# Gate and up projections from the third inner tile on by seven half-depth products instead of eight

## The chip, the cores and the metric

The kernel runs on one core of a Trainium2 chip. Times are device microseconds of one execution; the number that counts is the median of several executions. A profile of one further execution shows where its time went: TensorE (PE, and PEld for its weight loads), VectorE (DVE), ScalarE (ACT), GpSimd (POOL) and SyncE (SP, which only issues DMAs).

## What is computed

One transformer layer on 8 sequences of 128 tokens, width 512, all in float32:

```python
x = x + xattn(layernorm(x), ctx, ctx, mask, Wq, Wk, Wv, Wo)   # 32 heads, 8 kv heads of 128
x = x + ffn(layernorm(x), w1, w2, w3)

def ffn(x, w1, w2, w3):                     # w1, w2: [1376, 512], w3: [512, 1376]
    dq1, dq2, dq3 = (nf4_quant_dequant(w) for w in (w1, w2, w3))
    gate = einsum('bsd,hd->bsh', x, dq1)
    up = einsum('bsd,hd->bsh', x, dq2)
    return einsum('bsh,dh->bsd', silu(gate) * up, dq3)
```

`nf4_quant_dequant` scales each block of 64 weights by its largest absolute value, rounds to the nearest of 16 code values (15 bounds between them) and scales back. This quantizing is part of what the kernel computes.

## The kernel before

**Precision.** A float32 matrix product is made of three matmuls: each operand is split into a rounded high part (a cast on ACT, line 155) and a rest (a subtraction on DVE or POOL, line 156), and `product` (line 165) issues high x low, high x high and low x high for each 128-deep slice (line 172). A product over 512 input channels of a 128 x 512 result is thus 4 x 3 = 12 matmuls.

**The stages on PE.** First key and value projections and the first query projections (to about 118 us). Then 64 attention steps (line 762), a step being one sequence and one kv head with its four query heads. In each step PE does, in this order, a query product `pq` for a later unit, the output product `po` of three steps ago (line 700), the transposes of two steps ago (`turn`, line 696), the values of the step before (line 686) and this step's scores (line 675). From about 600 us on gate and up: for each of 11 tiles of the inner width (the last one padded) and each of 2 halves of the tokens, a product for gate and one for up (`gate_up`, line 730), then SiLU on ACT and a product on DVE (lines 751, 752) into `hT`. From 724 us on the down projection (line 872): for sequences 0 to 5 the inner tiles 0 to 7 first (`most`, 12 steps of 12 matmuls), then tiles 8 to 10 of these, then sequences 6 and 7. Its stationary operand `hs` is made from `hT` by `split_h` (line 841).

**The quantizing stream** runs beside all this. It is a Python generator (`quantize`, line 376) that issues the work of 17 units in order: 11 units of 128 x 1024 weights of w1 and w2 (`Up`), 5 such and one of 96 x 512 of w3 (`Down`). In a unit, each of the 15 bounds is a compare on ACT (line 196) and a sum on DVE into two PSUM banks (line 202); then a scaling on DVE. The next unit's weights are loaded by DMA some compares before the end (line 393) and normalized on POOL (line 206). `pump(n)` issues so many steps of the stream as its argument says, a step being 128 x 1024 wide; the calls stand by hand in the program (lines 645, 781, 799, 862, 886). What each engine then does, it does in the order in which the program issued it.

A finished `Up` unit leaves four 128 x 128 weight tiles in two stores: each splits 512 columns (ACT cast, POOL subtraction) and writes high and low part to DRAM (`store`, line 286). A finished `Down` unit leaves one or two w3 tiles that stay in SBUF (line 242). Such leftovers wait in a list and are issued one at a time by `store()` (line 411), once in each attention step, before its first `pump`. The gate/up tiles come back by DMAs from POOL's queue (`load_w12`, line 725) into six buffers that they share with the query weights and with `hs`.

**The order within an attention step** on ACT: two copies `rs_q` for the rope of the query product (lines 463, 464), the store's cast, the compares of `pump(1.5)`, the cast of the transposed values `aT`, tanh and exp of the scores (681, 682), the compares of `pump(1.65)`, the cast of a query or output weight tile. On DVE: the rope's product `rc_q` (465), sums of the first pump, `acc` (705), the rest of `aT`, reciprocal and scaling of the values (693, 694), sums of the second pump. On POOL: `rs_q`'s product (466), the store's subtraction, the mask product (684), the rope's sum (467), the subtraction of the weight tile.

**PSUM** has eight banks of 512 columns: two for the stream's sums, two (tag q) in turn for query products and transposes, two for the values, one for the scores, one for the output product.

Of the kernel before, what the change touches and what calls it, by code (L numbers as in the profile page):

```python
# [31 lines left out]
NG = 44  # L32

# [29 lines left out]
def block_kernel(ctx: ExitStack, tc: tile.TileContext, x, ctxt, mask, wq, wk, wv, wo, w1, w2, w3, w12t, w3_t,  # L63
# [6 lines left out]
    ps = ctx.enter_context(tc.tile_pool(name="ps", bufs=2, space=bass.MemoryType.PSUM))  # L70
    tp = ctx.enter_context(tc.tile_pool(name="tp", bufs=2))
    nf = ctx.enter_context(tc.tile_pool(name="nf", bufs=2))
# [7 lines left out]
    w12t_d = dram.tile([NHT, 2, P, 2, KT, P], F32, name="w12t_d")  # L80
# [31 lines left out]
    def rsqrt_apart(v, y, n, name):  # L112

        p = ps.tile([P, 1024], F32, tag="c", name=f"rp_{name}", bufs=1)
# [50 lines left out]
    def product(out, pairs, start=True, stop=True, high=False):  # L165


        n = len(pairs)
        for i, ((ah, al), (bh, bl)) in enumerate(pairs):
            three = [(ah, bh), (al, bh), (ah, bl)] if high else [(ah, bl), (ah, bh), (al, bh)]  # L170
            for j, (a, b) in enumerate(three):
                E.matmul(out, a, b, start=start and i + j == 0, stop=stop and i == n - 1 and j == 2)  # L172
# [11 lines left out]
    class Unit:  # L184
# [6 lines left out]
        def bound(self, i):  # L191
# [4 lines left out]
            S.activation(m, self.w, AF.Relu, bias=bias[:self.p, i:i + 1], scale=BIG if up else -BIG)  # L196
            step = float(NF4[i + 1] - NF4[i])
            if i == NEG[-1]:
                self.c = ps.tile([P, 1024], F32, tag="c", name=f"nc_{self.name}", bufs=1)[:self.p, :self.n]
# [48 lines left out]
    class Up(Unit):  # L248
# [30 lines left out]
        def finish(self):  # L279
            V.tensor_tensor(self.w, self.c, self.s, ALU.mult)  # L280
            for j, part in self.parts(self.w):
                for i in range(self.r // P):
                    fresh.append(lambda tag, h=self.start // P + i, j=j, src=part[:, :, i * P:(i + 1) * P]:
                                 self.store(h, j, src))

# [81 lines left out]
    ups = [Up((j,), h * P, 2 * P) for h in range(0, NHT - 1, 2) for j in range(2)] + [Up((0, 1), (NHT - 1) * P, P)]  # L367
# [8 lines left out]
    def quantize():  # L376
        invert = None
        for i, u in enumerate(units):
            for k, b in enumerate(NEG[::-1] + POS):
                u.bound(b)  # L380
# [9 lines left out]
                if k == 2:  # L390
                    u.begin()
                if i + 1 < len(units):
                    if k == (6 if isinstance(units[i + 1], Down) else 10):
# [23 lines left out]
    def end_store():  # L417
        if stored:
            stored.pop()()

# [6 lines left out]
    with ExitStack() as c1:  # L427
# [56 lines left out]
        with ExitStack() as c3:  # L484
# [61 lines left out]
            def masks():  # L546
# [5 lines left out]
                some = tp.tile([P, T], F32, tag="t_some", name="some", bufs=1)  # L552
# [6 lines left out]
                def count():  # L559
                    pa = bank("s", "pa")  # L560
# [162 lines left out]
        w12, hT, ups = {}, {}, []  # L723

        def load_w12(h):
            w12[h] = [wp.tile([P, 2, KT, P], F32R, tag="wq", name=f"w12_{h}_{j}", bufs=6) for j in range(2)]
            for j in range(2):
                nc.gpsimd.dma_start(w12[h][j], w12t_d[h, j])

        def gate_up(half, h, pool=None, between=None):  # L730
            t = xT2[half]
            pg, pu = bank("q", f"pg_{half}_{h}"), bank(("pv", "wo")[len(ups) % 2], f"pu_{half}_{h}")
            ups.append(h)

            def one(w, p):
                product(p, [((w[:, 0, k], w[:, 1, k]), (t[:, 0, k], t[:, 1, k])) for k in range(KT)])

            one(w12[h][0], pg)
            if between:
                between()  # L740
            one(w12[h][1], pu)
            if h % 4 == 0:
# [3 lines left out]
                else:  # L746
                    hT[half, h // 4] = pool.tile(shape, F32, tag="hT", name=name, bufs=4)

            def later():
                sg = tp.tile([P, 512], F32, tag="t1", name=f"sg_{half}_{h}")  # L750
                S.activation(sg, pg, AF.Silu)
                V.tensor_tensor(hT[half, h // 4][:, h % 4], sg, pu, ALU.mult)
# [9 lines left out]
        for i in range(N):  # L762
# [36 lines left out]
            pump(1.65 if 2 < i < 58 else 2 if i == 58 else 1 if i < 2 else 0)  # L799
# [7 lines left out]
            if i >= 61:  # L807
                load_w12(i - 61)
# [16 lines left out]
        evac = gate_up(0, 0, between=lambda: project(N - 1))  # L825
        ln.sums(7)
        turned((4, 5), ("s", "wo"))
        ln.finish()
        xn.update({k: ln.rows(k, "t2") for k in (6, 7)})
        evac()  # L830
# [100 lines left out]
```

## Time and profile before

| | |
|---|---|
| median of 3 executions | 789.2 us (789.14 to 790.14) |
| the profiled execution's own time | 790.0 us |
| its span, first to last instruction | 788.2 us |
| granted TensorE clock, mean | 0.998 |
| PE busy, share of the span | 778.0 us, 99% |
| DVE, ACT, POOL busy | 627.9 (80%), 586.4 (74%), 466.4 us (59%) |
| gate/up stage, third product to last | 614.9 to 723.6 us |
| down projection | 723.6 to 785.0 us |

The page gives busy time, number of instructions and, for groups of like instructions, total, mean length and the idle time before them with what ended it. Lengths of matmuls overlap in it, so the pace of PE is read from the starts of its weight loads. An engine runs its instructions in order; an instruction that waits holds up all behind it on its engine.

### The profile page before, as it was taken

The numbers are of one execution on the slowest core, as the hardware profiler recorded it, in microseconds if no ns is written. First come the engines' busy times: TensorE is split into PE (matmuls) and PEld (weight loads), VectorE is DVE, ScalarE is ACT, GpSimd is POOL, SyncE is SP. The second block draws the span as 40 slices with busy tenths as digits, with TensorE's granted clock in tenths as the row PEclk, the third lists the DMA queues.
The fourth block names the chain that finished last, engine by engine and source line by source line (L and its number), as shares of the span: only waits on it lengthen the run. The fifth ranks groups of instructions, "written<-read, shape, count | busy, mean of one in ns | idle before, by whom it ended". The sixth has DMA issues, their size and how long they took to land. (4 is left out here: it accounts for less than half of the span.)

```text
span 788.2 us, 11198 instructions
## 1 busy us (share of the span) xinstructions
PE 778.0 (99%) x3737; PEld 627.3 (80%) x3737; DVE 627.9 (80%) x840; ACT 586.4 (74%) x821; POOL 466.4 (59%) x411
## 2 busy tenths in 40 slices
PE   8999998999999999999999999999999999999998
PEld 6788886778777878778787877888778888888877
DVE  5767777888888887888888878879878688888981
ACT  7358667989796978879797979898732678778840
POOL 3568544688787878777797877878652223232100
PEclk9999999999999999999999999999999999999999
DMA  7966735355437344526337432414133235652011
GB/s 228 300 195 195 214 105 154 108 143 176 89 121 206 135 107 121 174 55 218 103 100 203 131 94 94 125 65 134 43 119 107 57 108 157 186 162 53 5 54 54
DMA packets 73329, 102.44 MB, mean 130 GB/s; under 512 B 7832, under 2 KB 42840, under 8 KB 73272
## 3 DMA queue, kind: packets, MB, share of 16 engines
q1 hardware_dynamic: 70104, 90.19, 38.2%
q0 software_dynamic: 3168, 11.54, 4.7%
q8 instruction: 30, 0.49, 0.3%
q14 instruction: 27, 0.22, 0.1%
HBM read 79.32 MB, written 22.38 MB: 129 GB/s over the span
## 5 line engine op out<-in xcount | busy, mean ns | idle before, releaser
L202 DVE SCALAR_TENSOR_TENSOR nc_w<-nm_w,nc_w 128x1024 f32<-128x1024 bf16 (+1 forms) x238 | 284.6, 1196 | 60.2 <-ACT nm_w L196 49.8
L196 ACT ACTIVATE nm_w<-w_w,bias 128x1024 bf16<-128x1024 f32 (+1 forms) x255 | 276.2, 1115 | 14.9 <-DVE nc_w L202 7.9
L172 PE MATMUL pq<-xT,wq 128*128 128x512 f32 x768 | 209.3, 422 | 0.0
L172 PE MATMUL po<-wo,aT 128*128 128x512 f32 x768 | 190.1, 396 | 0.0
L172 PEld LDWEIGHTS pq<-xT,wq 128*128 128x128 f32 x768 | 143.9, 188 | 55.9 <-issue 24.4
L172 PEld LDWEIGHTS po<-wo,aT 128*128 128x128 f32 x768 | 143.8, 189 | 34.5 <-issue 2.9
L684 POOL TENSOR_TENSOR th<-th,mt 128x512 f32<-128x512 f32 x64 | 83.8, 1310 | 87.9 <-ACT th L682 80.0
L466 POOL TENSOR_TENSOR rs_q<-rs_q,sgnq 128x512 f32<-128x512 f32 x64 | 82.9, 1295 | 14.7 <-ACT rs_q L464 14.7
L681 ACT ACTIVATE th<-pl 128x512 f32<-128x512 f32 x64 | 38.3, 598 | 53.5 <-PE pl L678 51.3
L467 POOL TENSOR_TENSOR qr<-rc_q,rs_q 128x512 f32<-128x512 f32 x56 | 72.5, 1295 | 0.0
L691 PE MATMUL pv<-vt,th 128*128 128x129 f32 x512 | 67.9, 276 | 0.1
L678 PE MATMUL pl<-qr,krt 128*128 128x512 f32 x128 | 66.4, 601 | 0.0
L172 PE MATMUL pg<-xT,w 128*128 128x512 f32 x264 | 63.7, 390 | 0.0
L172 PE MATMUL pu<-xT,w 128*128 128x512 f32 x264 | 63.5, 389 | 0.0
L691 PEld LDWEIGHTS pv<-vt,th 128*128 128x128 f32 x512 | 62.2, 192 | 0.7 <-POOL th L684 0.7
L172 PE MATMUL pd<-w3t,hs 128*128 128x512 f32 (+3 forms) x297 | 60.8, 366 | 0.4 <-POOL w3t L156 0.4
L172 PEld LDWEIGHTS pd<-w3t,hs 128*128 128x128 f32 (+1 forms) x297 | 51.3, 189 | 9.9 <-POOL w3t L156 0.8
L206 POOL TENSOR_TENSOR w_w<-w_w,s_w 128x1024 f32<-128x1024 f32 (+1 forms) x17 | 39.6, 2329 | 33.0 <-DMA s_w<-scale_d 31.6
L172 PEld LDWEIGHTS pu<-xT,w 128*128 128x128 f32 x264 | 49.6, 188 | 10.3
L172 PEld LDWEIGHTS pg<-xT,w 128*128 128x128 f32 x264 | 49.3, 188 | 10.1
L156 POOL TENSOR_TENSOR w3t<-w_w,w3t 128x512 fp32r<-128x512 f32 (+1 forms) x11 | 17.2, 1564 | 65.7 <-ACT w3t L155 65.7
L155 ACT CAST aT<-pt_a 128x512 fp32r<-128x512 f32 x64 | 36.6, 571 | 24.9 <-PE pt_a L162 24.9
(119 smaller groups left out, 1103.7 us busy)
## 6 DMA issues: line engine op xcount, KB each, us to landing
w12t_d<-dqt SPq DMA_DIRECT2D x22, 512.0 KB
w<-w12t_d POOLq DMA_DIRECT2D x22, 512.0 KB, 4.6
s_w<-scale_d SPq DMA_DIRECT2D x40, 256.0 KB
raw_wq<-in_L_xattn_Wq SPq DMA_DIRECT2D x32, 256.0 KB
raw_wo<-in_L_xattn_Wo SPq DMA_DIRECT2D x32, 256.0 KB
s_w<-scale_d SPq DMA_DIRECT2D x86, 64.0 KB
ws<-in_L_ffn_w SPq DMA_DIRECT2D x20, 256.0 KB
w_w<-in_w12t SPq DMA_DIRECT2D x10, 512.0 KB
```

What stands on the lines that cost most here:

```text
L155: S.copy(hi, src)
L156: engine.tensor_tensor(lo, src, hi, ALU.subtract)
L172: E.matmul(out, a, b, start=start and i + j == 0, stop=stop and i == n - 1 and j == 2)
L196: S.activation(m, self.w, AF.Relu, bias=bias[:self.p, i:i + 1], scale=BIG if up else -BIG)
L202: V.scalar_tensor_tensor(self.c, m, step, self.c, ALU.min, ALU.subtract if i == POS[0] else ALU.add)
L206: Q.tensor_tensor(self.w, self.w, self.s, ALU.mult)
L466: Q.tensor_tensor(s, s, every(sgn), ALU.mult)
L467: return lambda: (engine or Q).tensor_tensor(dst, c, s, ALU.add)
L678: E.matmul(pl, krt[kv, u % 2][:, bb * T:(bb + 1) * T], qr[u][:, bb].rearrange("p g t -> p (g t)"), start=True, stop=True)
L681: S.activation(th, pl, AF.Tanh, scale=ATTN_MULT / CAP)
L684: Q.tensor_tensor(em[i], em[i], mt.unsqueeze(1).to_broadcast([P, G, T]), ALU.mult)
L691: E.matmul(pv[:, g, :HD + 1], em[i][:, g], vt[kv][:, b], start=True, stop=True)
```

## The change

For tiles 2 to 10 of the inner width (`H0 = 2`), gate and up of both token halves are taken as one product of 2 x 2 blocks: rows are gate and up (w1 and w2), the inner dimension is cut into two halves of 256 input channels, columns are the two token halves. Instead of eight block products it makes seven (the scheme of Strassen in the form with few sums): P1 = A11 B11, P2 = A12 B21, P3 = S4 B22, P4 = A22 T4, P5 = S1 T1, P6 = S2 T2, P7 = S3 T3, where A are blocks of the weights, S sums of them, B blocks of the normalized tokens and T sums of them. Each block product has 2 x 3 = 6 matmuls. Tiles 0 and 1 stay as they were.

- **Weights.** The stream's `Up` units are recut: two for tiles 0 and 1 as before, then one unit for each tile with w1 and w2 together. After scaling, such a unit makes S1 to S4 with four DVE sums of 128 x 256 and leaves four stores, two of them with sums in front. A store writes one or two blocks. An attention step may issue a second store, ahead of its second pump, which is 1.7 instead of 1.65.
- **Tokens.** T1 to T4 are made and split once, on DVE, POOL and ACT, ahead of and beside the first products of the stage.
- **Results.** PSUM is laid out anew when the gate/up stage begins: two banks x, two v, one y, one z. Products add onto banks that ACT has filled by copies, so that most sums are made in PSUM; ACT makes four copies and two SiLUs a tile, DVE two sums and a product, POOL a product.
- **Loads.** Weight blocks are loaded one at a time by DMAs from SP's queue as buffers come free.
- **Stream.** In `Down` units three of the 15 compares go to POOL. Loads and second scale loads of a unit are issued at other compares. Each block product has `pump(0.74)`, and there are new pumps of 1.5 and 2.2 at the start of the stage.
- **Down.** `split_h` subtracts on POOL instead of DVE; the order of `most` is all sequences for tiles 0 to 3, then all for 4 to 7, and two of its steps come ahead of the last two block products.

The diff's core:

```diff
+H0 = 2
+PAIRS = [("A11", "S1"), ("S2", "A12"), ("S3",), ("A22", "S4")]
...
-        def bound(self, i):
+        def bound(self, i, engine=S):
...
+            if engine is S:
+                S.activation(m, self.w, AF.Relu, bias=bias[:self.p, i:i + 1], scale=BIG if up else -BIG)
+            else:
+                Q.tensor_single_scalar(m, self.w, float(BOUNDS[i]), op=ALU.is_gt if up else ALU.is_le)
...
             V.tensor_tensor(self.w, self.c, self.s, ALU.mult)
+            if len(self.js) == 2:
+                self.combine()
+                return
...
+        def combine(self):
+            a11, a12, a21, a22 = (self.w[:, i * 256:(i + 1) * 256] for i in range(4))
+            s1 = self.s[:, :256]
+            def first(tag):
+                V.tensor_tensor(s1, a21, a22, ALU.add)
+                self.store_blocks(s1, "S1")
+            def third(tag):
+                V.tensor_tensor(a21, a11, a21, ALU.subtract)
+                V.tensor_tensor(a11, a22, a21, ALU.subtract)
+                V.tensor_tensor(a12, a12, a11, ALU.subtract)
+                self.store_blocks(self.w[:, :512], "S2", "S4")
+            fresh.extend([first, lambda tag: self.store_blocks(self.w[:, :512], "A11", "A12"), third,
+                          lambda tag: self.store_blocks(self.w[:, 512:], "S3", "A22")])
+        def store_blocks(self, src, *names):
+            n = len(names)
+            t = nf.tile([P, 2, 2, 2 * P], F32R, tag="nf_t", name=f"dqs_{self.name}_{names[0]}")
+            split(t[:, :n, 0], t[:, :n, 1], src.rearrange("p (i n) -> p i n", i=n), Q)
+            for i, name in enumerate(names):
+                c, at = PLACE[name]
+                nc.sync.dma_start(w12s_d[self.start // P - H0, c][:, at].rearrange("p i k c -> p i (k c)"),
+                                  t[:, i].bitcast(F32))
...
-    ups = [Up((j,), h * P, 2 * P) for h in range(0, NHT - 1, 2) for j in range(2)] + [Up((0, 1), (NHT - 1) * P, P)]
+    ups = [Up((j,), 0, H0 * P) for j in range(2)] + [Up((0, 1), h * P, P) for h in range(H0, NHT)]
...
-                u.bound(b)
+                u.bound(b, Q if isinstance(u, Down) and k % 5 == 2 else S)
...
-                if k == 2:
+                if k == (2 if isinstance(u, Down) else 8):
                     u.begin()
                 if i + 1 < len(units):
-                    if k == (6 if isinstance(units[i + 1], Down) else 10):
+                    if k == (6 if isinstance(units[i + 1], Down) else 11):
                         units[i + 1].load()
...
-            pump(1.65 if 2 < i < 58 else 2 if i == 58 else 1 if i < 2 else 0)
+            if i > 3 and len(to_store) > 1:
+                store()
+            pump(1.7 if 2 < i < 58 else 2 if i == 58 else 1 if i < 2 else 0)
...
-        split(t[:, 0, :n], t[:, 1, :n], hT[b // 4, i][:, :, b % 4 * T:b % 4 * T + T], V)
+        split(t[:, 0, :n], t[:, 1, :n], hT[b // 4, i][:, :, b % 4 * T:b % 4 * T + T], Q)
...
+    Q.tensor_tensor(w11, plain(B11[0]), plain(B11[1]), ALU.add)
+    Q.tensor_tensor(t4, plain(B21[0]), plain(B21[1]), ALU.add)
+    V.tensor_tensor(t1, plain(b12[0]), w11, ALU.subtract)
+    V.tensor_tensor(t1, t1, plain(b12[1]), ALU.add)
+    V.tensor_tensor(t2, plain(B22[0]), t1, ALU.subtract)
+    V.tensor_tensor(t2, t2, plain(B22[1]), ALU.add)
+    def split_t123():
+        split(T1[0], T1[1], t1, Q)
+        V.tensor_tensor(w11, t2, w11, ALU.subtract)
+        split(T2[0], T2[1], t2, V)
+        Q.tensor_tensor(t4, t4, t2, ALU.subtract)
+        for k in range(2):
+            split(T3[0][k], T3[1][k], w11[:, k], Q)
+    def split_t4():
+        split(T4[0], T4[1], t4, Q)
...
+        def P1(self):
+            block(self.h, "A11", "B11", self.x)
+            def later():
+                S.copy(y, self.x)
+        def P5(self):
+            block(self.h, "S1", "T1", self.v)
+        def P6(self):
+            block(self.h, "S2", "T2", self.x, False)
+            return lambda: S.copy(self.h0, self.x)
+        def P2(self):
+            block(self.h, "A12", "B21", y, False)
+            def later():
+                self.sg = self.silu(y, "0")
+        def P7(self):
+            block(self.h, "S3", "T3", self.x, False)
+            def later():
+                S.copy(z, self.x)
+                S.copy(self.h1, self.x)
+                V.tensor_tensor(self.h1, self.h1, self.v, ALU.add)
+                V.tensor_tensor(self.v, self.v, self.h0, ALU.add)
+        def P4(self):
+            block(self.h, "A22", "T4", z, False)
+            return lambda: V.tensor_tensor(self.h0, self.sg, z, ALU.mult)
+        def P3(self):
+            block(self.h, "S4", "B22", self.v, False)
+            def later():
+                sg = self.silu(self.v, "1")
+                Q.tensor_tensor(self.h1, sg, self.h1, ALU.mult)
...
+    slots = [(H0, "P1"), (0, "both"), (1, "both"), (H0, "P2"), (H0, "P6"), (H0, "P5"), (H0, "P7")]
+    for h in range(H0, NHT):
+        slots += [(h + 1, "P1"), (h + 1, "P5"), (h, "P4"), (h + 1, "P6"), (h, "P3"), (h + 1, "P2"), (h + 1, "P7")]
+    slots = [k for k in slots if k[0] < NHT]
+    slots[-2:-2] = [(NHT, "down")]
...
+    most = [(b, i) for i in range(2) for b in range(6)]
+    down = most + [(b, 2) for b in range(6)] + [(b, i) for b in range(6, B) for i in range(3)]
...
+        store()
+        pump({"both": 2.2, "down": 3}.get(what, 0.74))
+        for _ in range(frees.get((h, what), 0)):
+            if chunks:
+                load_chunk()
+            elif to_split:
+                split_h(*to_split.pop(0))
```

## The prediction

> **What bounds the kernel now.** I read the page first: engine shares and the costliest groups.
>
> ```profile
> PE 778.0 (99%) x3737; PEld 627.3 (80%) x3737; DVE 627.9 (80%) x840; ACT 586.4 (74%) x821; POOL 466.4 (59%) x411
> L172 PE MATMUL pg<-xT,w 128*128 128x512 f32 x264 | 63.7, 390 | 0.0
> L172 PE MATMUL pu<-xT,w 128*128 128x512 f32 x264 | 63.5, 389 | 0.0
> ```
>
> PE is full, so matmuls taken away count in full where nothing else sets the end. The mean of 389 ns is a pipelined length. The timeline of the gate/up stage gives the true pace:
>
> ```profile
> 647.43 2.68 PEld L172 LDWEIGHTS pg<-xT,w 128*128 128x128 f32 x12
> 650.15 2.68 PEld L172 LDWEIGHTS pu<-xT,w 128*128 128x128 f32 x12
> 652.87 2.68 PEld L172 LDWEIGHTS pg<-xT,w 128*128 128x128 f32 x12
> ```
>
> Twelve matmuls start every 2.72 us: 0.2267 us each. Next, the chain of work that ended last:
>
> ```profile
> 747.48 9.23 issue
> 756.71 1.60 POOLq L927
> 758.35 26.69 PE pd L172 x147
> ```
>
> At 758.35 PE resumes because GpSimd has just split the last w3 tile. So the quantizing stream (ScalarE compares, VectorE sums, GpSimd splits) ends level with PE, and a faster PE meets it. Last, busy times by stretch (columns: PE, PE loads, DVE, ACT, POOL) and one attention step from the timeline:
>
> ```profile
> 160.00:560.00 400.00, 400.00 (x1983) 320.39 (x1982) 335.68 (x437) 339.66 (x480) 315.61 (x258) 1.00 0.43 127
> 408.75 0.63 ACT L682 ACTIVATE th<-th 128x512 f32<-128x512 f32 x1
> 409.29 2.17 ACT L196 ACTIVATE nm_w<-w_w,bias 128x1024 bf16<-128x1024 f32 x2
> 409.46 1.31 POOL L684 TENSOR_TENSOR th<-th,mt 128x512 f32<-128x512 f32 x1 [0.49 <-ACT th L682]
> 409.79 0.69 DVE L694 TENSOR_TENSOR ad<-pv,rs 128x512 f32<-128x512 f32 x1
> 410.72 1.30 POOL L467 TENSOR_TENSOR qr<-rc_q,rs_q 128x512 f32<-128x512 f32 x1
> 412.60 0.58 ACT L464 COPY rs_q<-pq 64x512 f32<-64x512 f32 x1
> 413.26 0.69 DVE L465 TENSOR_TENSOR rc_q<-pq,cosq 128x512 f32<-128x512 f32 x1 [0.24 <-ACT rs_q L464]
> 415.19 0.19 PEld L172 LDWEIGHTS pq<-xT,wq 128*128 128x128 f32 x1 [0.24 <-issue]
> ```
>
> A step lasts 7.68 us (exp at 401.09 and 408.75). ACT idles 60 us over the 52 steps of the stretch, 1.16 each. But its order is fixed: the next q product (415.19) needs the bank that rc_q leaves at 413.95, and rc_q follows ACT's copies. By this timeline ACT may be late by 1.24 us; over the other steps the distance from rc_q's end to the next q product is 1.2 to 2.4, mean 1.8.
>
> **The change, part by part.**
>
> Matmuls. A tile of the inner width took 4 products of 12 (two token halves, gate and up) = 48; now 7 blocks of 6 = 42. Nine tiles (2 to 10): 54 x 0.2267 = 12.24 us less PE work, if nothing waits.
>
> The end. PE begins the stage's third product at 614.88 in both. Then: 63 blocks x 1.36 = 85.7, two gate-and-up pairs of the old kind 10.9, twelve down steps x 2.72 = 32.6, the first two w3 tiles of the next step 1.36: PE wants the last w3 tile at 745.4. The stream has 11 x 16 + 5 x 16 + 8 + 15 = 279 units. Counting the pump calls, 259 are issued when the slots end (716.9 with two down steps in them); 20 remain, 12 of full size and 8 of the half-size last unit. VectorE needs 12 x 1.235 (full sums, back to back in the timeline) + 15 x 0.745 + 0.68 (the 96x512 ones) = 26.7 us. It can start at about 719.2, after the last SiLU (0.6), one hs cast (0.6) and one compare (1.14) on ACT: 745.9. Then the cast (1.1) and GpSimd's split (1.6) of the last w3 tile: 748.7. PE waits 3.3 us there, and the 147 matmuls behind are the same. Gain: 758.35 - 748.7 = 9.65 us instead of 12.24.
>
> What that end needs is freed elsewhere: hs subtractions go from DVE (24 x 0.69) to GpSimd, 18 compares from ACT (15 x 1.14 + 3 x 0.72 = 19.3 us) to GpSimd, which was busy 30.5 of 109 us in this stage. The trace has no one-source compare on GpSimd: per 1024 columns the memset takes 0.97 and the two-source product 2.40; I take 1.7, 18 x 1.7 = 31 us, hidden in its idle time.
> [...]
>
> Copies and sums in the gate/up stage, per tile: ACT four copies (4 x 0.58) more than its two SiLUs, DVE three sums instead of two (+0.69), GpSimd one product (1.3). With 5.2 units pumped per 9.52 us, ACT is busy some 8.4, DVE 8.4. Every copy has two blocks (2.72 us) before PE needs it; ACT reaches the copy for z about 1.6 late after two compares, so it fits narrowly. Bound: 0 to 10 us, of which the first 3.3 only replace the wait at the end. I take 0.
> Making the operands once (DVE 6 x 1.22, GpSimd about 15 us) has the two old pairs (10.9 us) and two blocks as cover; gone, it costs up to 3. Weight loads go from GpSimd's queue to SP's, single, with 8 blocks (10.9 us) from the freed buffer to the use. L728's median to landing is 4.6 us, at most 7.6, plus 8 scale loads ahead of it (4.25): 8.9 to 11.9. I take 0, up to 1 for each of 10 bursts.
>
> The attention stage: **here is the price.** The dequantized blocks are now combined for tiles 2 to 10. Each of nine units leaves four stores: S1 (one DVE sum), A11/A12, then "third" (three DVE sums, each needing the one before), S3/A22. Counting the calls, S1 is issued in the second half of a step in 8 of 9 units, and third too: after exp, mask and rope sum, before the compares. There ACT's cast waits for the sums at the head of ACT's queue. Behind it stand the compares, the wq/wo cast and the rs_q copies, for which DVE's rc_q and PE's next q product wait.
>
> These sums read both operands from SBUF, and so do GpSimd's products. What that does, the rows show (tile views, min/median/max, and a timeline pair):
>
> ```profile
> L467 DVE TENSOR_TENSOR kr<-rc_k,rs_k x6: 693/1277/1291, 16.0 to 31.8; 128x512 f32<-128x512 f32 x6
> 124.81 2.39 DVE L156 TENSOR_TENSOR wo<-raw_wo,wo 128x512 fp32r<-128x512 f32 x2
> 125.12 1.53 POOL L466 TENSOR_TENSOR rs_q<-rs_q,sgnq 128x512 f32<-128x512 f32 x1 [2.08 <-ACT rs_q L464]
> ```
>
> The same sum takes 0.69 alone and 1.28 beside a GpSimd product, whose end it awaits; of the two wo sums, the second waits for the GpSimd product that slipped in after the first. 256 columns alone: 0.41 (0.684 for 512 and 0.548 for 384 of hs, on a line). So in a step, from exp's end: GpSimd's mask product runs to 1.38, the first sum ends at 1.8, GpSimd's rope sum runs to 3.1, the second ends at 3.5, the third at 3.9 (GpSimd's next instruction waits for ACT's cast). The cast adds 0.6: ACT is 4.5 late. For S1: 1.8 + 0.35 = 2.2 late.
> Off goes the mean tolerance of 1.8: S1 costs 0.4, third 2.7 plus what is left of S1's lateness a step earlier, about 0.3 of it. 3.4 us a unit, 9 units: **+30.6 us**.
> Low end: no GpSimd wait. DVE is free 0.85 after exp in the median; third 0.85 + 1.23 + 0.6 = 2.7 late, costs 0.9; S1 nothing: 8 us. Fully absorbed: 0. High end: tolerance 1.2 everywhere: 1.0 + 3.3 + 0.4 = 4.7, 9 units: 42. I take the middle one, because every row with a GpSimd product beside it shows the wait.
> [...]
>
> Other added work there: casts 4 for 2 per unit (+0.96 us ACT, +1.9 GpSimd, per five steps) and pump 1.7 for 1.65: ACT 6.53 to 6.77 of 7.68 a step, hidden. The load of a unit moves one compare later in the previous one, and four scale loads replace two (0.6 each on SP): GpSimd may wait up to 2 us for its normalizing; the mask product has 4.4 - 1.4 = 3.0 us before PE's next values product needs it. I take 0, up to 1 a unit.
>
> Sum against the profiled execution (790.0; span 788.2 and 1.8 around it): 790.0 - 9.6 + 30.6 = 811.0. The median is 0.8 below that execution: **810**.
>
> **Rivals.**
> Not slower: ACT's waits in the attention fall into idle it has anyway (1.16 x 5 = 5.8 us a unit against 1.8 + 3.9 = 5.7 of waits). Place: the two casts of a unit. Then only the end counts: 789.2 - 9.6 = 779.6. It decides from 9.6 / 9 = 1.07 us lost per unit downward. For it: the sums match almost exactly. Against: the idle is spread in pieces of about 1 us, the tolerance is 1.8, third needs 4.5 at once.
> The gain doesn't appear: the stream, not PE, sets the end. If DVE falls 10 us further behind in the gate/up stage, the last w3 tile comes at 758 as now: 789. For it: DVE at 8.4 of 9.52. Against: from 600 to 627 it is busy only 17.7 of 27 us, and the change pumps there.
> Both losses: attention at its high end and waits on z, the weights or the operands (5 to 10): 789.2 - 9.6 + 42 + 7 = 829.
>
> **How the numbers follow.** Forecast 0.57 (its own range 793 to 822), absorbed 0.30, no gain 0.08, both losses 0.05. A difference within 0.2% is about what a measurement of this kernel can't tell from none. No gain splits into 0.05 same, 0.02 slower, 0.01 faster; so faster 0.31, same 0.05, slower 0.64. The range runs from 778 to 825; outside it lie the last case, the forecast's tail and the lowest part of the absorbed one.
>
> **What would show it.** Right: in the list of waits, ACT's casts of the S1 and S2/S4 tiles waiting for DVE by 1 to 4 us, up to 18 times; DVE sums of 128x256 at 0.4 to 1.7 us; steps of 7.7 us with one of 10 to 11 in five; PE idle or matmuls of pq and po stretched. The stage from the third product to the down steps 12 us shorter; PE waiting some 3 us for the last w3t split. Wrong: steps of 7.7 throughout, or PE stretched in the gate/up blocks.

## The result, and the profile after

The changed kernel takes **882.1 us** (median of 4 runs, 880.5 to 882.9), the kernel before 789.5 on the same chip (4 runs, 789.1 to 790.1): ratio 1.117, 95% interval 1.115 to 1.119. The forecast was 810, its range 778 to 825. The sign was right; the size, 20.8 us more forecast against 92.6 measured, was wrong by a factor of more than four.

The page of the changed kernel, engine shares and the row of the clock granted to TensorE (40 slices, in tenths):

```profile
PE 798.4 (91%) x3683; PEld 629.1 (71%) x3683; DVE 656.3 (75%) x867; ACT 599.3 (68%) x862; POOL 576.6 (65%) x471
...
PEclk9999999999998999999999999899999899999969
```

The 54 matmuls are gone (3737 to 3683), yet PE is busy 20 us longer, at 91% of a longer span: it waits, and part of the time it runs slowly. The trace's record of the clock has 69.6 us at half speed, against 4.1 before (1.4 and 0.7 of it behind the last instruction). The span of 880.9 us, cut at marks that both traces have (us):

| stretch | before | after | more | forecast |
|---|---|---|---|---|
| to the last score product | 589.6 | 654.8 | 65.2 | 30.6 |
| to the first gate product | 9.9 | 10.3 | 0.4 | 0 |
| to the stage's third product | 15.5 | 26.8 | 11.3 | 0 |
| from there to the last w3 tile | 143.5 | 156.0 | 12.5 | -9.6 |
| the rest | 29.8 | 33.1 | 3.3 | 0 |

**Attention.** The list of waits (us in total, times, longest):

```profile
PEld pq L181 <- DVE rc_q L511: 34.8, 15, 4.4
ACT dqs_w_S L164 <- DVE w_w L316: 31.4, 8, 4.0
...
PEld pd L181 <- POOL w3t L165: 17.0, 3, 11.9
POOL w_w L220 <- DMA s_w<-scale_d: 16.1, 6, 8.2
...
ACT dqs_w_S L164 <- DVE s_w L310: 15.1, 7, 3.9
```

The second and the last row are the two casts that the prediction named: 3.9 us each before S2/S4 (31.4 / 8), 2.2 each before S1 (15.1 / 7). The first row is PE's wait behind them. One unit's third store in the timeline:

```profile
226.24 0.63 ACT L728 ACTIVATE th<-th 128x512 f32<-128x512 f32 x1
...
228.20 1.29 POOL L513 TENSOR_TENSOR qr<-rc_q,rs_q 128x512 f32<-128x512 f32 x1
228.43 1.35 DVE L314 TENSOR_TENSOR w_w<-w_w 128x256 f32<-128x256 f32 x1
229.88 0.43 DVE L315 TENSOR_TENSOR w_w<-w_w 128x256 f32<-128x256 f32 x1
...
230.34 0.42 DVE L316 TENSOR_TENSOR w_w<-w_w 128x256 f32<-128x256 f32 x1
...
230.84 0.62 ACT L164 CAST dqs_w_S<-w_w 128x512 fp32r<-128x512 f32 x1 [3.96 <-DVE w_w L316]
...
233.46 0.60 ACT L164 CAST wo<-raw_wo 128x512 fp32r<-128x512 f32 x1
...
235.29 0.69 DVE L511 TENSOR_TENSOR rc_q<-pq,cosq 128x512 f32<-128x512 f32 x1 [0.18 <-ACT rs_q L510]
...
236.03 4.17 PEld L181 LDWEIGHTS pq<-xT,wq 128*128 128x128 f32 x12 [4.35 <-DVE rc_q L511]
236.03 4.61 PE L181 MATMUL pq<-xT,wq 128*128 128x512 f32 x12 [3.52 <-DVE rc_q L511]
```

Read it downwards: the exp ends at 226.87, VectorE reaches the three sums 1.6 us later, and the first is stretched to 1.35, against 0.43 for the second, beside GpSimd's rope sum of 1.29; the cast is 3.96 late; behind it stand two compares, the wo cast, the copies; then rc_q, and only then PE, idle for 3.52. The last line is what the prediction didn't have: twelve matmuls in 4.61 us where the same place in e5 shows 3.06, since the granted clock was 0.50 from 236.4 to 239.8.

Take the attention step by step (counted from 0, from one score product to the next, each against the same step before). The 65.2 us lie like this: the nine steps in which PE meets a third store's wait lost 45.3, the nine of S1 9.6, all others 10.3 (7.9 of it in steps 50 and 51).

**The end.** The chain of work that ended last:

```profile
820.10 2.77 POOL nm_w L210
847.82 29.80 PE pd L181 x147
```

Before, ScalarE's compares and VectorE's sums led up to the last w3 tile, at 758.4; now a compare on GpSimd stands in the chain, and the 147 matmuls behind take 29.8 instead of 26.7: the clock's record has a half-clock spell from 833.8 to 854.2, whose last 6.4 us lie over them.

### The profile page after: what moved, and what is told of

It is laid out like the page before. It is cut to its first block, busy times and chain, and to the rows that moved or that the text cites. A ratio compares the mean times of both kernels' runs of the same rounds, so it can differ in the third digit from the quotient of the medians.

```text
span 880.9 us, 11467 instructions
## 1 busy us (share of the span) xinstructions
PE 798.4 (91%) x3683; PEld 629.1 (71%) x3683; DVE 656.3 (75%) x867; ACT 599.3 (68%) x862; POOL 576.6 (65%) x471
## 4 chain that ended last, share of the span: by engine, by line
PE 51%; DVE 17%; ACT 14%; POOL 7%; issue 6%; DMA 3%; SPq 2%; DVEq 0%; ACTq 0%; POOLq 0%
PE po L181 11%; PE pq L181 10%; ACT nm_w L207 7%; DVE nc_w L216 6%; PE pvp L181 5%; PE pd L181 4%; PE pk L181 3%; PE pv L737 3%; PE px L181 3%; PE pl L724 3%; PE pv L181 2%; POOL nm_w L210 2%; PE pt_a L171 2%; ACT rs_q L510 1%; DVE acc L751 1%
## 5 line engine op out<-in xcount | busy, mean ns | idle before, releaser
L207 ACT ACTIVATE nm_w<-w_w,bias 128x1024 bf16<-128x1024 f32 (+1 forms) x237 | 260.0, 1121 | 21.2 <-DVE nc_w L216 12.8
L181 PE MATMUL pq<-xT,wq 128*128 128x512 f32 x768 | 213.4, 429 | 23.5 <-DVE rc_q L511 23.4
L181 PEld LDWEIGHTS pq<-xT,wq 128*128 128x128 f32 x768 | 148.9, 196 | 85.4 <-DVE rc_q L511 34.8
L181 PE MATMUL po<-wo,aT 128*128 128x512 f32 x768 | 195.3, 404 | 14.3 <-DVE acc L751 14.2
L181 PEld LDWEIGHTS po<-wo,aT 128*128 128x128 f32 x768 | 144.6, 192 | 55.3 <-ACT th L728 11.3
L181 PE MATMUL pd<-w3t,hs 128*128 128x512 f32 (+3 forms) x297 | 65.4, 382 | 15.4 <-POOL w3t L165 15.4
L511 DVE TENSOR_TENSOR rc_q<-pq,cosq 128x512 f32<-128x512 f32 x60 | 41.3, 689 | 18.5 <-ACT rs_q L510 17.9
L210 POOL TENSOR_SCALAR nm_w<-w_w 128x1024 bf16<-128x1024 f32 (+1 forms) x18 | 46.1, 2560 | 11.7 <-DVE nc_w L216 10.8
L165 POOL TENSOR_TENSOR wq<-raw_wq,wq 128x512 fp32r<-128x512 f32 x32 | 41.1, 1285 | 14.3 <-ACT wq L164 13.9
L220 POOL TENSOR_TENSOR w_w<-w_w,s_w 128x1024 f32<-128x1024 f32 (+1 forms) x17 | 39.6, 2331 | 16.3 <-DMA s_w<-scale_d 16.1
L181 PE MATMUL pk<-cT,wk 128*128 128x512 f32 x192 | 48.1, 398 | 1.8 <-DVE rc_k L511 0.9
L181 PE MATMUL pvp<-wv,cT 128*128 128x512 f32 x192 | 46.2, 393 | 0.0
```

The source lines that it names most:

```text
L165: engine.tensor_tensor(lo, src, hi, ALU.subtract)
L210: Q.tensor_single_scalar(m, self.w, float(BOUNDS[i]), op=ALU.is_gt if up else ALU.is_le)
L220: Q.tensor_tensor(self.w, self.w, self.s, ALU.mult)
L511: V.tensor_tensor(c, src4, every(cos), ALU.mult)
```

## The experiments

Each run is one profiled execution beside one of the kernel before on the same chip (789.2 to 789.9 us). "Last score" is the start of the last score product, 589.6 before and 654.8 after. Diffs are against the changed kernel unless said otherwise. A single run leaves differences of a few us open: attention steps 50 and 51, with the same code, lost 3.8 us together in e7, 0.0 in e9, 2.2 in e13 and 0.0 in e14.

### e1: without the sums

```diff
-                V.tensor_tensor(s1, a21, a22, ALU.add)
...
-                V.tensor_tensor(a21, a11, a21, ALU.subtract)
-                V.tensor_tensor(a11, a22, a21, ALU.subtract)
-                V.tensor_tensor(a12, a12, a11, ALU.subtract)
```

(S1 to S4 then hold whatever lies there, so this kernel's output isn't the layer's.)

> Leaves out the four VectorE sums of every combined unit (S1 to S4 are then stored as whatever lies there; all casts, stores, transfers, products and the pump stay). Theory 'sums at the head of ScalarE's queue': their waits cost the attention 65 us together with the half-clock windows that the PE gaps bring on; without them the last score product starts at 590 to 600 in place of 654.7, the half-clock time falls from 70 us to under 35, and the run takes 812 to 828 us. Rival 'more work': casts, stores, scale loads and a pump of 1.7 fill the engines; then the last score product stays after 640 and the run takes 865 us or more.

Measured: 835.6 us, last score at 608.9, half-clock time 44.6 us. 46 of the 65 us go with four small sums. More work as the whole cause falls; but all three numbers miss the theory's ranges, and 19 us stay that the sums don't explain.

### e2: the sums on GpSimd

```diff
-                V.tensor_tensor(s1, a21, a22, ALU.add)
+                Q.tensor_tensor(s1, a21, a22, ALU.add)
```

(and the other three likewise)

> The same four sums on GpSimd in place of VectorE; all else as in the changed kernel. If the price is the chain (three dependent sums ahead of the cast, wherever they run), GpSimd needs about 0.65 a sum by half its 128x512 sums of 1.3, plus its own queue: the third store's cast still waits 2.5 to 4 us, and the run takes 850 to 885 us. If the price is VectorE and GpSimd shutting each other out of SBUF, the cast waits about 2 us and the run takes 825 to 845 us.

Measured: 900.2 us, slower than either expectation. Waits of ScalarE:

```profile
ACT dqs_w_S L164 <- POOL w_w L316: 44.1, 9, 5.0
...
ACT dqs_w_S L164 <- POOL s_w L310: 29.3, 9, 3.6
```

A sum takes 0.73 there, but stands behind GpSimd's mask and rope products; the cast waits 4.9 instead of 3.9. Taking VectorE out of GpSimd's way doesn't help: the length of the chain ahead of the cast counts, whoever makes it.

### e3: the sums ahead of their casts

```diff
+            s2, s4 = self.s[:, 256:512], self.s[:, 512:768]
+            V.tensor_tensor(s1, a21, a22, ALU.add)
+            def one(tag):
+                self.store_blocks(s1, "S1")
+                V.tensor_tensor(a21, a11, a21, ALU.subtract)
+            def two(tag):
+                self.store_blocks(self.w[:, :512], "A11", "A12")
+                V.tensor_tensor(s2, a22, a21, ALU.subtract)
+            def three(tag):
+                self.store_blocks(self.w[:, 512:], "S3", "A22")
+                V.tensor_tensor(s4, a12, s2, ALU.subtract)
+            fresh.extend([one, two, three, lambda tag: self.store_blocks(self.s[:, 256:768], "S2", "S4")])
...
-                if k == (2 if isinstance(u, Down) else 8):
+                if k == (11 if isinstance(u, Up) else 6 if u is units[len(ups)] else 2):
                     u.begin()
```

(by the lines on `begin` a unit of w1 and w2 loads its second scale tile later, at compare 11 instead of 8)

> The same sums on VectorE, each issued one store (half a step) ahead of the cast that reads it, into places of their own (S1, S2 and S4 in the free scale tile, S3 in place); the scale tile is loaded three compares later for that. Amount of work unchanged. Theory 'sums at the head of ScalarE's queue': the casts no longer wait, the last score product starts at 592 to 605, and the run takes 815 to 835 us. [...]

Measured: 838.8 us, last score at 612.0, half-clock time 42.5; both times lie just above the theory's ranges. The same place in the timeline:

```profile
227.18 1.27 DVE L322 TENSOR_TENSOR s_w<-w_w,s_w 128x256 f32<-128x256 f32 x1
...
230.84 0.69 DVE L515 TENSOR_TENSOR rc_q<-pq,cosq 128x512 f32<-128x512 f32 x1
...
231.57 2.68 PEld L181 LDWEIGHTS pq<-xT,wq 128*128 128x128 f32 x12 [0.48 <-DVE rc_q L515]
```

The sum is as long as before (1.27, beside GpSimd), but ScalarE doesn't stand at a cast for it: PE's weight loads wait 0.48 instead of 4.35. The same sums in another place are worth 43 us of the whole. In the attention, the steps with S1's and third stores' waits lose 6.1 us instead of 54.9, 48.8 less; the other steps lose 6 more than in the changed kernel, nearly all in steps 17, 34 and 50. GpSimd waits more for scales here (27.8 us against 16.1, and 24.6 in e1), and e3 asks for a scale tile later. e3 lies 3 us above e1, which has no sums; what their own work costs can't be told apart from that later load.

### e4: the 18 compares back on ScalarE

```diff
-                u.bound(b, Q if isinstance(u, Down) and k % 5 == 2 else S)
+                u.bound(b, S)
```

> The 18 compares of the last six units that the change gave to GpSimd are back on ScalarE. Attention as in the changed kernel (last score product at 654 to 656). Theory 'GpSimd is too slow for its new part (2.56 a compare, 46 us)': PE's waits for w3 splits at the end (15.4 us) fall to 8 or less, and the run takes 868 to 876 us. Rival 'ScalarE has no room for them beside the four copies a tile': PE waits in the blocks for py, pz and the SiLUs, 5 us or more, and the run takes 880 us or more.

Measured: 860.8 us, 21 less, and faster than expected. From the third product to the last w3 tile 145.4 instead of 156.0; the wait for w3 splits 6.5 instead of 15.4; the last score came 9 us earlier, which the expectation had at nothing: the first GpSimd compares stand in the attention (from 599.9 us), and 7.6 of the 9 come back in its steps 56 to 58. In the changed kernel, the compare on GpSimd and on ScalarE (min/median/max in ns):

```profile
L207 ACT ACTIVATE nm_w<-w_w,bias x237: 707/1144/1164, 55.3 to 841.4; 128x1024 bf16<-128x1024 f32 x113, 96x512 bf16<-96x512 f32 x6
L210 POOL TENSOR_SCALAR nm_w<-w_w x18: 1483/2774/2802, 599.9 to 840.5; 128x1024 bf16<-128x1024 f32 x15, 96x512 bf16<-96x512 f32 x3
```

and what that does at the end:

```profile
835.99 1.49 POOL L210 TENSOR_SCALAR nm_w<-w_w 96x512 bf16<-96x512 f32 x1
837.52 3.88 DVE L216 SCALAR_TENSOR_TENSOR nc_w<-nm_w,nc_w 96x512 f32<-96x512 bf16 x5 [3.51 <-POOL nm_w L210]
...
847.82 1.65 PE L181 MATMUL pd<-w3t,hs 96*128 96x512 f32 x3 [11.16 <-POOL w3t L165]
```

The compare stands behind splits and hs subtractions on GpSimd's queue, VectorE waits 3.5 us for it, and the last w3 tile behind them is late. ScalarE had room for the 18.

### e5: the two adds at the start of the gate/up stage

```diff
-    Q.tensor_tensor(w11, plain(B11[0]), plain(B11[1]), ALU.add)
-    Q.tensor_tensor(t4, plain(B21[0]), plain(B21[1]), ALU.add)
+    V.tensor_tensor(w11, plain(B11[0]), plain(B11[1]), ALU.add)
...
+        Q.tensor_tensor(t4, plain(B21[0]), plain(B21[1]), ALU.add)
         Q.tensor_tensor(t4, t4, t2, ALU.subtract)
```

> The changed kernel with one edit: of the two whole-operand adds that GpSimd does while VectorE still makes the last layer norms, one goes to VectorE behind the norms, the other to GpSimd behind T1's split. Theory 'GpSimd's adds shut VectorE out of its small norm instructions': from the first gate product to the stage's third product 26.8 us become 17 to 20, the 10 us half-clock window there goes, and the run takes 868 to 875 us. Rival 'the pumped normalizing does it, or the five sums of the operands themselves': 24 us or more stay, and 878 us or more.

Measured: 874.6 us; from the first gate product to the stage's third 20.9 instead of 26.8, a little more than the theory's 20. (2.1 of the 7.5 us come from the attention, whose code is the same.) What had happened in the changed kernel:

```profile
670.96 2.40 POOL L943 TENSOR_TENSOR whole<-xT 128x1024 f32<-128x1024 f32 x1 [7.61 <-PE po L181]
...
673.32 2.39 POOL L944 TENSOR_TENSOR whole<-xT 128x1024 f32<-128x1024 f32 x1
673.42 2.33 DVE L109 TENSOR_SCALAR i_y<-v_y 128x2 int32<-128x2 int32 x1
...
675.68 2.37 POOL L220 TENSOR_TENSOR w_w<-w_w,s_w 128x1024 f32<-128x1024 f32 x1
675.78 2.30 DVE L110 TENSOR_SCALAR y_y<-i_y 128x2 int32<-128x2 int32 x1
...
681.53 1.12 PE L171 MATMUL pt_y<-ident,xn_y 128*128 128x128 f32 x4 [4.33 <-DVE xT L165]
```

and in e5, with a place in the attention that is wanted below:

```profile
236.04 2.63 PEld L181 LDWEIGHTS pq<-xT,wq 128*128 128x128 f32 x12 [4.35 <-DVE rc_q L511]
236.05 3.06 PE L181 MATMUL pq<-xT,wq 128*128 128x512 f32 x12 [3.52 <-DVE rc_q L511]
...
670.61 0.17 DVE L109 TENSOR_SCALAR i_y<-v_y 128x2 int32<-128x2 int32 x1
670.82 0.17 DVE L110 TENSOR_SCALAR y_y<-i_y 128x2 int32<-128x2 int32 x1
```

A VectorE instruction on two columns takes 0.17 us in e5, where no GpSimd instruction runs beside it, and 2.33 beside a GpSimd instruction of 2.39, whose end it awaits; the next one (2.30) meets the unit's normalizing (2.37) in the same way. The two adds stand behind VectorE's norms in the program, but once released at 670.96 GpSimd ran all three back to back; the norms, on which PE waited (4.33 us), stood still.

### e6: the three repairs together

e3, e4 and e5 in one kernel.

> Sums ahead of their casts, compares back on ScalarE and the moved adds together. If the three losses are separate, they add up: 882 less 43 (sums ahead), less 12 (the part of the compares' 21 that lies behind the attention), less 7 to 11 (adds): 816 to 820 us, with the last score product at 612. If they share one cause (half-clock windows that come anyway), the sum falls short by 10 us or more: 828 us and above.

Measured: 824.3 us, last score at 606.5. 58 of the 92 us are gone; the sum falls short by 4 to 8 us, between the two expectations. The shortfall has a place of its own: from the last score product to the first gate product this run took 15.5 us instead of 10.3. There one normalization on VectorE took 5.74 us instead of 0.54, and PE waited 3.74 for it; the last section shows the same in e9. So the three losses do look separate.

### e7: the scales asked for earlier

```diff
-                    if k == (6 if isinstance(units[i + 1], Down) else 11):
+                    if k == (6 if isinstance(units[i + 1], Down) else 9):
                         units[i + 1].load()
```

(the second scale load at compare 9 too, and one DMA for w1 and w2 together)

> As the three repairs, and a combined unit's scales and weights are asked for two compares earlier, its scales by two DMAs in place of four. What is left of the attention's loss (22 us) sits in steps where GpSimd waits 5 to 10 us for a unit's scales. Theory 'recut units ask for their scales too late': 8 to 15 us less than the three repairs, the last score product at 597 to 604, 801 to 810 us in all. Rival 'the scales arrive when the queues let them': within 3 us of the three repairs.

Measured: 815.6 us, last score at 599.0: 8.7 less than e6, as the theory had it. Of this, 3.7 lie in steps 17, 34 and 39, which lost only 0.1 us in the changed kernel (2.6 in e1, 4.0 in e6, 0.2 here): a loss that came up with the repairs. Steps 50 and 51 went from 8.5 to 3.8. GpSimd's wait for scales, first e6, then e7:

```profile
POOL w_w L220 <- DMA s_w<-scale_d: 25.3, 9, 9.8
```

```profile
POOL w_w L220 <- DMA s_w<-scale_d: 6.9, 5, 3.0
```

The worst in e6 was the last combined unit: eight writes of w3's scale table stood on SP's queue ahead of its loads, its normalizing waited 9.8, and PE 6.2 for the mask product queued behind it.

### e8 and e11: filling PE's gaps

Both are the changed kernel with the waiting q product made once more, unused, just ahead of itself; e8 in the bank "s", e11 in "wo" (`third_at` holds the step in which a third store was issued).

```diff
+            if third_at == [i - 1]:
+                w, t = wqt[(u + 1) // 2, tiles[0]], xT[(u + 1) % 2]
+                product(bank("s", f"fill_{i}"), [((w[:, 0, k], w[:, 1, k]), (t[:, 0, k], t[:, 1, k])) for k in range(KT)])
             later = [q_proj(u + 1, g) for g in tiles]
```

> The changed kernel, with the q product that waits behind each third store computed once more into another bank just before it (12 matmuls, result unused), so that TensorE has 2.7 us of work in the 3.5 us gap; the waits of ScalarE's casts stay. Theory 'the half clock follows the gap': the windows behind those seven stores go, and a third-store step loses 4.0 to 4.3 us where it lost 5.2 to 6.4 (filled gaps do not cost more, since TensorE was waiting there); the last score product starts 6 to 12 us earlier, at 643 to 649, and the run takes 870 to 876 us. Rival 'the half clock comes from elsewhere': the windows stay where they are, the extra product adds up to 2.7 us a unit, 882 us or more.

> As e8, with the unused product in the bank of the output projection, which is read about 1 us after the scores: in e8 the extra product had to wait 2.2 to 3.5 us for its bank (for the tanh), so the gap was not filled but moved. Now TensorE should idle at most 1.2 us before it and about 1 us behind it, the casts of the third stores waiting as in the changed kernel. Theory 'the half clock follows the gap': none of the seven third-store steps has a half-clock window and each loses 4.0 to 4.4 us; the last score product at 643 to 650. Rival 'it comes from elsewhere': windows remain in three or more of these steps.

Measured: 881.5 and 892.8 us. Neither filled the gap. The filler waited for its own bank, in e8 for ScalarE's tanh (up to 3.5 us), in e11 for VectorE:

```profile
PEld fill L181 <- DVE acc L751: 33.4, 8, 5.5
```

so the gap stood in front of the filler, and half-clock windows lie within 10 us of five of the eight fillers in e8 and of six in e11. That is what the rival forecast, but as the gaps stayed, it decides nothing on whether the clock follows the gap; the comparison and the table of gaps below bear on that.

### e9, e10, e12 to e15: can the gain be had

e9: on e7, the operands are split after the copies and SiLUs that PE waits for, T3 ahead of T4, 1.5 compares moved into the attention's last steps. The diff's core:

```diff
-            ahead, later = later, [split_t123]
+            ahead, later = later, []
...
-            later += ahead
+            later += ahead + [split_t123]
```

> As e7, with the operands of the products made later than the copies and SiLUs that TensorE waits for, T3 ahead of T4 on GpSimd, the second w3 unit's normalizing moved ahead of the last layer norms, and the SiLU before the compares. In e7 TensorE waits 4.1, 3.0, 4.2, 1.3 and 3.7 us at these places, and 6.8 at the end for the last w3 split. Theory 'each wait is the order's own': 10 to 14 us of the first five go and the wait at the end grows by 0 to 4, for VectorE sets it: 802 to 810 us. Rival 'the work itself is too much for VectorE': what goes here comes back at the end, 812 us or more.

Measured: 812.6 us, just inside the rival's range. The start became 2.4 us shorter (17.0 from the first gate product to the third of the stage), but the wait moved on: 3.7 us for a SiLU and 3.3 for a copy, both behind casts and compares on ScalarE.

e10: e9 with `pump(1.75)` for 1.7.

> As e9, with 0.05 more compares per attention step (2.75 in all). If VectorE sets the end, the last wait shrinks by 2.75 x 1.23 = 3.4 us and the attention loses 1 at most: 2 to 3.5 us below e9. If the attention has no room: the same as e9 or slower.

Measured: 817.1 us, 4.4 slower than e9. The last wait fell from 6.2 to 3.3, but the last score came 6.1 later, one step with 5.2 us and a half-clock window among it, and the stretch from the third product to the last w3 tile took 4.5 more (from the last score to the first gate product it took 5.8 less, since the long normalization didn't come). Slower, as the second expectation had it: the attention has no room for more.

e12: e9 with 0.8 instead of 2.2 compares beside each of the two old pairs, 0.79 instead of 0.74 beside each block, and a w3 unit's normalizing at compare 10 instead of 13.

> As e9, with the third w3 unit's... normalizing of a w3 unit three compares earlier, and 0.8 compares in place of 2.2 beside each of the two old gate-and-up pairs (0.05 more beside every later block), since VectorE and ScalarE are full there while TensorE waits 4.3 and 4.4 us for a SiLU and a copy. Theory 'too much of the stream stands in the wrong place': 5 to 10 us less than e9, 802 to 808 us. Rival 'VectorE's total sets the end': the wait for the last w3 split grows by what is gained: 809 to 813 us.

Measured: 808.1 us, at the edge of the theory's range. But the gain isn't where the theory put it: it lies ahead of the first gate product (9.8 us after the last score instead of 15.6, without the long normalization), and from the third product to the last w3 tile both runs take 148.5. The waits of e9 at the start of the stage are gone, but a new one of 6.3 us appears, again behind a cast at the head of ScalarE's queue, here for GpSimd's sum of T4:

```profile
644.96 1.04 ACT L164 CAST xT<-whole 128x1024 fp32r<-128x1024 f32 x1 [3.93 <-POOL whole L968]
...
649.06 2.90 PE L181 MATMUL px<-T,w_S 128*128 128x512 f32 x6 [6.25 <-POOL xT L165]
```

e13: e12 with that sum on VectorE and the cast one block later.

```diff
-        Q.tensor_tensor(t4, t4, t2, ALU.subtract)
+        V.tensor_tensor(t4, t4, t2, ALU.subtract)
...
-        if (h, what) == (H0, "P2"):
+        if (h, what) == (H0, "P5"):
```

> As e12, with T4's second sum on VectorE instead of GpSimd and T4's cast one block later, since in e12 ScalarE stood 3.9 us before that cast and TensorE 6.3 us for the copy behind it. Theory 'order': the wait goes, and from the third product to the last w3 tile 148.5 us become 141 to 144; 800 to 804 us. Rival 'VectorE and ScalarE are the bound': the last wait (7.1 us) grows by as much; 806 to 809 us.

Measured: 804.6 us; from the third product to the last w3 tile 142.6 instead of 148.5, as the theory had it: order.

e14: e13 with `pump(0.88)` beside each block instead of 0.79.

> As e13, with 0.88 compares in place of 0.79 beside each block (5 to 6 compares more before the last down steps). Theory 'the end wait is a matter of place, for VectorE idles about a fifth of the block stage': the last wait falls from 7 to 0 to 2 us, the blocks lose at most 2; 795 to 800 us. Rival 'no room': the blocks lose what the end gains, within 2 us of e13.

Measured: 802.0 us. The 6.2 us wait for the last w3 tile is gone, but PE now waits 3.2 earlier in the down steps and the blocks lost 3.2: the same stretch took 143.9, 1.3 more than in e13. What is gained in all comes from the attention, whose code is the same in both, and from a half-clock window less behind the last tile. That is nearer to the rival than to the theory: no room in this stretch.

e15: e14 with one compare moved from the attention's last steps to the start of the stage.

> As e14, with one compare moved from the last attention steps to the start of the gate-and-up stage. In e12 the attention step that took it lost 3.4 us. Theory 'that step has no room for it': 1 to 3 us less than e14. Rival 'it is paid where it goes': the same as e14 within 1 us.

Measured: 800.7 us, 1.3 less by the time and 0.3 by the span; the time alone would fit the theory, but the step that lost 3.4 still loses 3.3. The rival again. No version beat the kernel before. The stretch from the third product to the last w3 tile, before, after and in e15 (columns: length, then busy time of PE, PE loads, DVE, ACT, POOL; granted clock):

```profile
614.88:758.35 143.47, 143.10 (x633) 118.17 (x631) 124.07 (x127) 112.96 (x135) 36.49 (x32) 1.00 0.35 100
```

```profile
691.86:847.82 155.96, 135.15 (x577) 109.07 (x577) 120.90 (x119) 113.13 (x151) 105.47 (x62) 0.94 0.43 137
```

```profile
624.43:768.60 144.17, 135.14 (x576) 108.43 (x576) 122.91 (x122) 125.16 (x167) 68.20 (x46) 0.99 0.47 149
```

PE works 8 us less and idles 9 us more. In e15 VectorE is busy 85% of the stretch and ScalarE 87%, before 86% and 79%. The gain in matmuls turned into idle time of PE. That it must, since the products' copies, sums and casts have to be threaded through two nearly full engines, is argued and not shown: VectorE was as full before, when PE had no gaps there.

## Why the prediction was wrong, by its steps

**Right: the place, and nearly the waits.** The forecast put the loss on the two casts, 2.2 and 4.5 us late with the cast, that is 1.8 and 3.9 before it; the waits are 2.2 and 3.9. e3 shows the place to be the cause. That 3.9 fits is partly luck. The forecast let the third store's first sum wait for GpSimd's mask product and the second for its rope sum; over the nine units the first sum takes 1.06 in the median, the second and the third 0.43 and 0.42, and in the rows above VectorE's own work holds them back for 1.6 us. Right too: the pace of the blocks (most tiles come round every 9.57 us against 9.52).

**Wrong: "Off goes the mean tolerance of 1.8".** This is the step that failed first. The cost of a third store is 4.0, 4.0 and 3.3 us in the three steps with no half-clock window (forecast 2.7 and 0.3), of an S1 step 0 to 2.3, mean 1.1 (forecast 0.4): about 4.8 a unit against 3.4, or 44 for nine, above the forecast's high end of 42. So a cast that comes 4.5 us late loses up to 4.0: the step absorbs about 0.5, and a mean over other steps (1.8, lowest 1.2) says nothing of it. The rival "not slower", by which ScalarE's idle time absorbs the waits, fails in the same place.

**Missing: the clock.** No term had it, though the trace before has a half-clock window of 3.4 us, at 130.7, behind its one gap of 2.4. The price can be read without an experiment of its own: e5's attention is the changed kernel's, and in the step shown above PE idled 3.52 us in both; in the changed kernel the clock then fell and the loads of twelve matmuls took 4.17 us, in e5 it didn't and they took 2.63. The step lost 5.39 and 4.50. So a window of 3.4 us cost 0.9 there. The attention has nine such windows more than before: some 8 us, an estimate. In e3, where these gaps are gone, it has one spell instead of eight. Of the 69.6 us at half speed, 20.5 are one spell around the wait for the last w3 tile and in the matmuls behind it, which the forecast had as "the same" and which took 3.1 us more.

**Mis-sized: "four scale loads replace two ... I take 0, up to 1 a unit".** The last two combined units (steps 50 to 58) lost 21.9 us. Without the cast waits 13.2 of these remain (e3), with the compares off GpSimd as well 8.4 (e6), with earlier scale loads 3.8 (e7), and in e9, with the same code there, nothing. So the late scales cost some 5 to 8 us, nearly all in one unit, the one whose loads stand behind the eight writes.

**Wrong: "making operands ... gone, it costs up to 3".** The stretch lost 11.3. The work was costed, the collision wasn't: GpSimd's adds ran as soon as they were released, which was in the middle of VectorE's norms (e5: 5.9 back; all of it but 1.6 in e9 to e15).

**Wrong: the GpSimd compare at 1.7, "hidden in its idle time".** It takes 2.77, more than the two-source product at 2.40. Idle time on average doesn't hide a link of a chain; forecast -9.65, measured +12.5, of which e4 takes back 10.6. The rest of the stretch's loss, 9 us by subtraction (12.5 more, with 12.2 of matmuls less and 15.4 of waits at the end), lies ahead of the down steps: PE took 22.6 us for the first 72 matmuls, 16.3 at the pace before, and lost 2.3 in the eight tiles after them. The forecast had "copies and sums" at 0 there, within a bound of 10.

**The rival "both losses"** had the right kind, and 829 was too little. "The gain doesn't appear" was right about the stage itself: with every repair made, the stretch takes as long as before (144.2 us against 143.5).

**Still open:** 8 us in e15's attention, lost in steps of 0.5 to 3.3 with more compares and casts on ScalarE; and whether another order of copies and casts could bring the stretch near the 131 us that its 576 matmuls need at the pace before (0.2267 us each). No run reached that.

## What to carry to other kernels

An instruction that waits at the head of an in-order queue costs what stands behind it, in that very step (a cast 4.5 us late lost up to 4.0 here): take the tolerance of the step where it lands, not a mean, and issue what it waits for half a step ahead (43 us here, with no work removed). Work that is given to an engine "with idle time" is hidden only if nobody waits for it; ask what it stands behind and whom it locks out (0.17 us became 2.33 above), and take its duration from the same operation, not from its neighbours. And where TensorE is at 99%, count a gap of 3 us as a gap and, more often than not, a slow spell after it: here 48 of the 61 gaps of 2.4 to 3.4 us were followed by one.

## What the runs showed of the hardware

**Gaps and the clock.** In the 17 traces, after the first 30 us, there are 106 spells of half clock, each a multiple of 3.413 us (in the changed kernel one to six times that, up to 20.48). All begin within 3.5 us of the end of a TensorE gap of at least 1.8 us, or inside it. Spells cut off by the end of the record are left out. By the gap's length, of gaps that begin at full clock: 1.2 to 1.8 us, 0 of 52 were followed by one; 1.8 to 2.4, 11 of 27; 2.4 to 3.0, 29 of 37; 3.0 to 3.4, 19 of 24; 3.4 and more, 48 of 50. Within each trace the spells begin whole multiples of 3.413 us apart.

**GpSimd's one-source compare** with bf16 output takes 2.77 us for 128 x 1024 and 1.49 for 96 x 512, longer than its two-source product (2.40 and 1.29).

**VectorE was held over several GpSimd instructions.** In e9 the second of two normalizations of 128 x 512, which mostly take 0.54 each, took 5.74, until GpSimd's run of DMA issues, a mask product, more DMA issues and a normalizing was over:

```profile
599.34 1.29 POOL L790 DMA_DIRECT2D w<-w12t_d  x2
599.43 6.21 DVE L159 TENSOR_SCALAR xn_y<-acc,mv_y,y_y 128x512 f32<-128x512 f32 x2 [0.74 <-POOL y_y L119]
...
600.65 1.29 POOL L741 TENSOR_TENSOR th<-th,mt 128x512 f32<-128x512 f32 x1
...
603.00 2.35 POOL L220 TENSOR_TENSOR w_w<-w_w,s_w 128x1024 f32<-128x1024 f32 x1
```

The same happened in e6 and e7 (5.74 each), with 15.5 and 16.0 us from the last score product to the first gate product, and in no other run; which of GpSimd's instructions did it, these runs don't tell.
